# A transformer layer stack on one core: the products for the memory gates laid by token tiles on 32-column strips of the array, with the gates as a block diagonal

## The chip, the core and the metric

The kernel runs on one core of a Trainium2 chip. A core has five engines that work side by side, each on its own in-order queue of instructions: TensorE (PE in the profile; PEld are its weight loads), VectorE (DVE), ScalarE (ACT), GpSimd (POOL) and SyncE (SP), which here only issues DMAs. They share an on-chip memory of 128 partitions, and TensorE writes its products into a second memory, PSUM, from which the other engines read. The metric is the device time of one execution in microseconds; the median of three runs of the kernel before is 1268.3 us.

## The reference

x has 8 batches of 512 tokens with 256 features. Four blocks follow each other, each with a layernorm ahead of it and a residual sum behind it: attention with a memory term, a feed-forward block, a retention block, the feed-forward block again.

```python
x = x + attn_a(layernorm(x))
x = x + ffn(layernorm(x))
x = x + attn_b(layernorm(x))
x = x + ffn(layernorm(x))
```

The change is in the first block. Its attention has 16 heads of 16 features, keys and values from a latent of 64 features, rope on queries and keys, and a decay by distance inside the softmax. What matters here is the memory term:

```python
memory_k = mean(k, axis=2)                     # one key per head
memory_v = mean(v, axis=2)                     # one value per head
memory_scores = einsum('bhqd,bhkd->bhqk', q, memory_k)
out = out + 0.2 * sigmoid(memory_scores) * memory_v
... out @ Wo + bo
```

For each batch there are thus 16 gates per token (one per head), and 16 memory rows, one per head, which are multiplied by Wo once.

## The kernel before

The work of one batch is cut into the front (layernorm, latent, keys, queries, values, the memory), the attention itself, and the rest (Wo, feed-forward, retention, feed-forward). All arithmetic is in 32-bit floats; a matmul is two rows of the trace.

**The attention** runs in 256 score steps, 32 per batch: a step makes the scores of a query tile of 128 tokens for two heads (s, in score_item) and VectorE takes their row maxima (mr); twelve steps later (LAG) the transposed scores (t, in prob_item) are made, ScalarE takes the exponential into p, and VectorE or GpSimd multiplies p by the decay table dec_a (soft_item; one pair of instructions a step). The products with the values (pv, in pv_item) have 128 rows and 32 columns of the array each, four heads side by side. Two score banks of PSUM (ps_sc) serve s and t, three others (ps_m) all other products.

**The memory.** mean_k (L533) puts the mean key into kmean as 16 columns, one per head. gate (L540) multiplies kmean by the rotated queries: two products of 512 columns each, one for each half of the rope, into rows 0 to 15 of a bank, and takes a tanh into the gates (a sigmoid is half of 1 + tanh). mean_v (L443) scales vmask, which has a column per head and one column of ones, by the mean value into vmean; through_wo (L458) multiplies it by Wo into mem, whose row 16 carries all that doesn't depend on a token: the output bias, and half of the memory rows. In the gates, row 16 is a constant 1, loaded once from the rope table. In wo_unit (L733), the product of gates and mem is the third product of each token tile, after the two of the attention's output with Wo:

```python
for c in range(NC):
    mm(ps[:, e * D : (e + 1) * D], aT[b][:, c, cols], wo_sb[:, c, :], c == 0, False)
mm(ps[:, e * D : (e + 1) * D], gates[b % 2][:, cols], mem[b % 2], False, True)
```

It has 128 rows of the array, of which only 17 hold anything but zeros.

**The order.** Ahead of the loop, the setup is written out by hand (from L1026). From there a planner (plan, L1072) decides when each piece comes. Each piece is a Unit with the time that it is booked for on TensorE and on the engines behind it; gate is Unit(gate, 1720, (("ACT", 600),)). The planner walks through the score steps with a clock for each engine, chooses at each point a step, a pair of value products or a Unit, and sums up the gaps of TensorE. It does so for all combinations of six rules (L1393: among them how long the decay product waits for GpSimd rather than go to VectorE, and how many steps earlier a front begins), takes the cheapest, and only then emits instructions, all engines in program order. In the first 64 steps it fills a gap of TensorE of over 700 ns with matmuls on the identity (warm), whose result nobody reads:

```python
if t < 2 * PER and gap > 700 and banks[0] <= clock["PE"] and not any(spare[i] for i in ts):
    n = min(20, (gap - 300) // 109)
    ...
    if emit:
        warm(n)
```

So a Unit's cost can change the order of the whole kernel. The decay product is given to GpSimd or VectorE by the line `pooled[i] = on <= own + (lead if i < EARLY else bias)` (L1232), where lead and bias are two of the rules.

## Time and profile before

| | us |
|---|---|
| three runs | 1267.91, 1268.30, 1269.02 |
| the profiled execution, its own time | 1267.68 |
| its span in the trace | 1265.9 |
| ACT busy | 499.4 |
| DVE busy | 615.4 |
| POOL busy | 763.6 |
| warm (fill) matmuls, 152 rows, length of one row, median | 0.275 |
| ga: 32 rows (8 gates), start to end of one row, median | 0.592 |
| tanh of a gate on ScalarE, 16x512, median | 0.587 |
| wo from me and ga: 64 rows, one row, median | 0.379 |

A row of the trace that gives a matmul's length counts from its start to its end, and the next one begins before it has ended; what a matmul costs is read from start to start. The span is what the trace covers; the device time lies some 1.8 us above it. Busy times of engines overlap, so they don't sum to the span.

### The profile page before, as it was taken

The numbers are of one execution on the slowest core, as the hardware profiler recorded it, in microseconds if no ns is written. First come the engines' busy times: TensorE is split into PE (matmuls) and PEld (weight loads), VectorE is DVE, ScalarE is ACT, GpSimd is POOL, SyncE is SP. The second block draws the span as 40 slices with busy tenths as digits, with TensorE's granted clock in tenths as the row PEclk, the third lists the DMA queues.
The fourth block names the chain that finished last, engine by engine and source line by source line (L and its number), as shares of the span: only waits on it lengthen the run. The fifth ranks groups of instructions, "written<-read, shape, count | busy, mean of one in ns | idle before, by whom it ended". The sixth has DMA issues, their size and how long they took to land.

```text
span 1265.9 us, 15939 instructions
## 1 busy us (share of the span) xinstructions
PE 1225.4 (97%) x6168; PEld 628.8 (50%) x6168; DVE 615.4 (49%) x995; ACT 499.4 (39%) x746; POOL 763.6 (60%) x699
## 2 busy tenths in 40 slices
PE   7989999999998999999999999999999999999999
PEld 5423445344534344455443644535543554467777
DVE  4777854573544663345734365433634372232410
ACT  2245444444453434334335245343434334523131
POOL 4379965795766876676657576675656564731210
PEclk9999999999999999999999999999999999999999
DMA  5310010002100100010000200011000100000000
GB/s 136 117 39 23 23 38 6 14 7 56 29 14 5 49 23 18 18 48 23 1 14 5 66 22 14 1 31 41 4 5 14 31 5 5 26 1 1 1 5 30
DMA packets 32728, 31.94 MB, mean 25 GB/s; under 512 B 14065, under 2 KB 23538, under 8 KB 32372
## 3 DMA queue, kind: packets, MB, share of 16 engines
q1 hardware_dynamic: 31740, 30.13, 8.7%
q8 instruction: 49, 0.80, 0.3%
q10 hardware_dynamic: 912, 0.79, 0.2%
q14 instruction: 27, 0.22, 0.1%
HBM read 13.92 MB, written 4.43 MB: 14 GB/s over the span
## 4 chain that ended last, share of the span: by engine, by line
PE 88%; DVE 6%; POOL 2%; DMA 2%; ACT 1%; issue 1%; SPq 0%; ACTq 0%; DVEq 0%
PE hx L203 19%; PE s L203 18%; PE x L203 18%; PE pv L203 8%; PE wo L203 3%; PE bs L203 3%; PE bo L203 3%; DVE mr L69 3%; PE b L203 2%; PE bv L203 2%; PE q L203 2%; POOL p L69 2%; PE t L203 2%; PE warm L203 1%; PE lat L203 1%; PE ga L203 1%
## 5 line engine op out<-in xcount | busy, mean ns | idle before, releaser
L69 POOL TENSOR_TENSOR p<-p,dec_a 128x512 f32<-128x512 f32 x482 | 610.0, 1290 | 296.5 <-ACT p L69 290.1
L69 DVE TENSOR_REDUCE mr<-s 128x2 f32<-128x1024 f32 x256 | 312.7, 1223 | 314.0 <-PE t L203 291.6
L69 ACT ACTIVATE p<-t 128x1024 f32<-128x1024 f32 (+1 forms) x282 | 263.0, 944 | 366.0 <-PE t L203 356.3
L203 PE MATMUL s<-kT,qT 32*128 32x512 f32 x1024 | 289.3, 640 | 19.5 <-DVE mr L69 17.0
L203 PE MATMUL t<-qT,kT 32*128 32x512 f32 x1024 | 287.2, 641 | 0.5 <-ACT p L69 0.3
L203 PE MATMUL x<-w_sb,h_x 128*128 128x256 f32 x960 | 221.0, 384 | 0.0
L203 PEld LDWEIGHTS x<-w_sb,h_x 128*128 128x128 f32 x960 | 178.3, 190 | 59.4 <-issue 36.4
L203 PEld LDWEIGHTS s<-kT,qT 32*128 32x128 f32 x1024 | 78.0, 183 | 162.0 <-DVE mr L69 62.9
L203 PE MATMUL pv<-p,va 128*32 128x512 f32 x1024 | 132.8, 608 | 1.6 <-ACT num L69 0.7
L69 ACT ACTIVATE h_x<-hx,vec 128x512 f32<-128x512 f32 (+1 forms) x128 | 84.5, 660 | 109.2 <-PE hx L203 108.3
L203 PE MATMUL hx<-xT_f,w_sb 128*128 128x512 f32 (+1 forms) x288 | 122.1, 560 | 0.2 <-ACT xT_f L69 0.2
L203 PE MATMUL hx<-xT_g,w_sb 128*128 128x512 f32 (+1 forms) x288 | 122.0, 560 | 0.0
L69 DVE TENSOR_TENSOR x<-x,x 128x256 f32<-128x256 f32 x60 | 25.5, 425 | 153.2 <-PE x L203 145.7
L203 PEld LDWEIGHTS t<-qT,kT 32*128 32x128 f32 x1024 | 78.6, 183 | 14.2 <-ACT p L69 5.4
L203 PEld LDWEIGHTS hx<-xT_g,w_sb 128*128 128x128 f32 x288 | 51.2, 189 | 64.0 <-issue 60.1
L203 PEld LDWEIGHTS hx<-xT_f,w_sb 128*128 128x128 f32 x288 | 50.8, 189 | 64.3 <-issue 55.3
L203 PEld LDWEIGHTS pv<-p,va 128*32 128x32 f32 x1024 | 25.3, 109 | 77.1 <-issue 51.5
L69 POOL TENSOR_TENSOR x<-x,b 128x256 f32<-128x256 f32 x60 | 43.9, 754 | 14.7 <-DVE xn_g L69 11.6
L69 POOL TENSOR_TENSOR rc<-rc,rs 128x512 f32<-128x512 f32 x30 | 40.2, 1361 | 9.2 <-DVE rs L69 9.2
L69 DVE TENSOR_TENSOR p<-p,dec_a 128x512 f32<-128x512 f32 x30 | 35.7, 1227 | 18.1 <-ACT p L69 18.1
L69 POOL TENSOR_TENSOR rstd_g<-ve_g,half 128x2 f32<-128x2 f32 x16 | 11.3, 704 | 54.0 <-DVE ve_g L69 53.8
L69 ACT COPY num<-pv 128x512 f32<-128x512 f32 x32 | 18.7, 585 | 57.9 <-PE pv L203 53.4
(172 smaller groups left out, 1103.0 us busy)
## 6 DMA issues: line engine op xcount, KB each, us to landing
kT<-rc SPq DMA_DIRECT2D x64, 64.0 KB
qT<-rc SPq DMA_DIRECT2D x60, 64.0 KB
x<-in_x_dram SPq DMA_DIRECT2D x7, 512.0 KB
aT<-num SPq DMA_DIRECT2D x112, 32.0 KB
rec<-d_rec SPq DMA_DIRECT2D x14, 256.0 KB
out_dram<-x SPq DMA_DIRECT2D x28, 128.0 KB
w_sb<-in_w_dram SPq DMA_DIRECT2D x2, 1024.0 KB
x<-in_x_dram SPq DMA_DIRECT2D x2, 256.0 KB
```

The source lines that it names most:

```text
L69: ins = f(*a, **k)
L203: tc.keep_in_program_order(nc.tensor.matmul(o, lhsT=l, rhs=r, start=start, stop=stop))
```

## The change

The products for the gates are cut by token tiles. For each half of the rope and each of the four tiles of 128 tokens there is one product with kmean, which now has 32 columns, and the result of tile t goes to partitions 32t to 32t+31 of the bank, its columns to 0 to 127. The tanh is taken tile by tile into the gates so that tile t stands in rows 32t to 32t+31 and columns 128t to 128t+127: a block diagonal, zero elsewhere. The memory's rows stand in mem four times, at rows 32t, so that the product in wo_unit (unchanged) still finds its gates and rows. For this, vmask, vmean and bo_row repeat their content four times, and vmean's scaling covers 128 columns instead of 17. The row of ones comes from the tanh itself: a bias of 40 in row 16 of each strip (one_rows, made from a table that lies in memory) gives tanh(40) = 1; the two loads of the gates' row of ones go. bo_row is loaded into four rows. mem needs no zeros beforehand, since its addition now writes all 128 rows. pick, which is only used at the start, moves to a buffer of the p pool. The Unit of the gate is booked with 620 ns on TensorE and 900 on ScalarE.

```diff
-    bo_row = keep([32, D], "bo_row")
-    kmean = keep([P, 2, P], "kmean")
+    one_rows = keep([P, 4], "one_rows")
+    bo_row = keep([P, D], "bo_row")
+    kmean = keep([P, 2, 32], "kmean")
-    vmask = keep([P, NC, NH + 1], "vmask")
+    vmask = keep([P, NC, NT, 32], "vmask")
...
             gps.memset(gates[i], 0.0)
-            gps.memset(mem[i], 0.0)
...
         gps.tensor_scalar(hmask, hmask, 0.5 / T, None, ALU.mult)
+        for t in range(1, NT):
+            gps.tensor_copy(vmask[:, :, t, :NH], vmask[:, :, 0, :NH])
...
-        for i in range(2):
-            move(gates[i][NH : NH + 1, :], rope[HD : HD + 1, 0, :])
+        move(one_rows, blocks[:, P : P + 4])
...
-        move(bo_row[NH : NH + 1, :], rows[D : 2 * D].unsqueeze(0))
+        move(bo_row[NH:P:32, :], rows[D : 2 * D].partition_broadcast(NT))
...
-    pick = keep([P, 2, 32], "pick")
+    pick = at.tile([P, 2, 32], F32, tag="p", bufs=PB, name="pick")
...
-                gps.tensor_scalar(vmean[:, c, : NH + 1], vmask[:, c, :], m[:, c : c + 1], None, ALU.mult)
+                gps.tensor_scalar(vmean[:, c, :], vmask[:, c].rearrange("p t h -> p (t h)"), m[:, c : c + 1], None, ALU.mult)
...
-            dve.tensor_add(mem[b % 2][: NH + 1, :], ps[: NH + 1, :D], bo_row[: NH + 1, :])
+            dve.tensor_add(mem[b % 2], ps[:, :D], bo_row)
...
             for e in range(2):
-                mm(ps, kmean[:, e, :], rot[0, e], e == 0, e == 1)
-            act.activation(gates[b % 2][:NH, :], ps[:NH, :], AF.Tanh)
+                for t in range(NT):
+                    mm(
+                        ps[t * 32 : t * 32 + 32, :P], kmean[:, e, :], rot[0, e][:, t * P : (t + 1) * P],
+                        e == 0, e == 1,
+                    )
+            for t in range(NT):
+                own = slice(t * 32, t * 32 + 32)
+                act.activation(gates[b % 2][own, t * P : (t + 1) * P], ps[own, :P], AF.Tanh, bias=one_rows[own, 0:1])
...
-        ga = Unit(gate, 1720, (("ACT", 600),), after=[km, qt], needs=(("wo", b - 2),))
+        ga = Unit(gate, 620, (("ACT", 900),), after=[km, qt], needs=(("wo", b - 2),))
...
-    gps.tensor_copy(vmean[:, :, NH], bvc)
+    gps.tensor_scalar(one_rows, one_rows, 40.0, None, ALU.mult)
+    dve.reduce_sum(one_rows[:, 0:1], one_rows, axis=AX.X)
+    for t in range(NT):
+        gps.tensor_copy(vmean[:, :, t * 32 + NH], bvc)
```

More of the change, by code (lines that the diff above doesn't have):

```diff
@@ L167, in memory_buffers @@
         gps.memset(vmask, 0.0)
-        gps.memset(vmask[:, :, NH : NH + 1], 1.0)
+        gps.memset(vmask[:, :, :, NH : NH + 1], 1.0)
         gps.memset(kmean, 0.0)
@@ L174, in masks @@
             dve.reduce_sum(
-                vmask[:, c, c * HH : (c + 1) * HH], ident.rearrange("p (h d) -> p h d", d=HD), axis=AX.X
+                vmask[:, c, 0, c * HH : (c + 1) * HH], ident.rearrange("p (h d) -> p h d", d=HD), axis=AX.X
             )
         gps.tensor_scalar(hmask, hmask, 0.5 / T, None, ALU.mult)
+        for t in range(1, NT):
+            gps.tensor_copy(vmask[:, :, t, :NH], vmask[:, :, 0, :NH])
     late = {}
@@ L455, in bias_through_wo @@
                 mm(ps[:, :D], vmean[:, c, :], wo_sb[:, c, :], c == 0, c == NC - 1)
-            dve.tensor_add(bo_row[: NH + 1, :], ps[: NH + 1, :D], bo_row[: NH + 1, :])
+            dve.tensor_add(bo_row, ps[:, :D], bo_row)
         def through_wo():
```

## The prediction

> **What bounds the kernel now.** I read the page first: the engines' shares, then the chain of waits.

> ```profile
> PE 1225.4 (97%) x6168; PEld 628.8 (50%) x6168; DVE 615.4 (49%) x995; ACT 499.4 (39%) x746; POOL 763.6 (60%) x699
> ...
> PE 88%; DVE 6%; POOL 2%; DMA 2%; ACT 1%; issue 1%; SPq 0%; ACTq 0%; DVEq 0%
> ```

> TensorE is busy 97% of the span and owns 88% of the chain, so a microsecond taken off it should be a microsecond of the total. But the share is a mean over stages, so I cut the span at the score steps (one score tile each, 256 in all, read from the row maxima on VectorE): step 12 at 57 us, step 48 at 161, step 74 at 272, last step at 1087.

> ```profile
> 57.40:95.00 37.60, 31.18 (x162) 10.18 (x154) 28.38 (x31) 16.52 (x31) 28.89 (x26) 0.95 0.13 33
> 95.00:130.00 35.00, 32.52 (x193) 11.00 (x194) 27.93 (x35) 18.64 (x33) 31.89 (x28) 1.00 0.11 29
> 130.00:161.00 31.00, 30.18 (x183) 13.15 (x182) 24.19 (x28) 15.89 (x30) 27.84 (x22) 1.00 0.07 18
> 161.00:272.00 111.00, 108.33 (x573) 51.13 (x571) 62.59 (x107) 47.51 (x65) 76.36 (x69) 1.00 0.07 17
> 272.00:1134.00 862.00, 847.26 (x4250) 412.88 (x4249) 407.47 (x647) 356.26 (x492) 565.83 (x503) 1.00 0.08 21
> ```

> The columns are the stretch, its length, and busy time of PE, PEld, DVE, ACT and POOL. From 161 us on TensorE is idle 2%. In the three front rows it is idle 6.4 + 2.5 + 0.8 = 9.7 us of 103.6, and POOL (88.6) and DVE (80.5) are nearly as loaded: there the engines pace each other. The waits of TensorE name the maxima on VectorE first (17.0 us, 22 times, for the next score tile).

> **The gates' products.** The third view is the timeline of TensorE around one gate.

> ```profile
> 332.71 0.59 PE L203 MATMUL s<-kT,qT 32*128 32x512 f32 x2
> 332.72 0.59 PE L203 MATMUL t<-qT,kT 32*128 32x512 f32 x2
> 333.24 1.98 PE L203 MATMUL ga<-rc,kmean 128*128 128x512 f32 x4
> 335.16 1.92 PE L203 MATMUL pv<-p,va 128*32 128x512 f32 x16
> ```

> A gate holds the array 1.92 us (333.24 to 335.16): two products, two rows each. Eight cost 15.4 us. Afterwards a gate is 8 products of 128 columns, 16 rows, in the shape of pv (128 rows, 32 columns), where four lie side by side: 16 pv rows of 512 columns take 1.86 us, so four at once take 0.46. A quarter of the columns is 0.12, four rounds 0.46, and entering a new shape costs 0.2 (a lone pair hx of 4 rows takes 1.91 us, 8 rows in a row 3.63). That gives **0.65 us**. Ends: 0.43 (pure streaming), and 16 x 0.112 = 1.8 if the four tiles run one after the other. The floor on issue is the nearest row with such small tiles:

> ```profile
> 4.81 0.84 PE L203 MATMUL qk_bias<-vec,pick 128*32 128x1 f32 x32
> 5.58 0.38 PE L203 MATMUL warm<-ident 128*128 128x128 f32 x1
> ```

> 32 rows in 0.77 us are 24 ns each, 16 make 0.39, less than the streaming. [...] The row is for the same tile shape, so I take 24 ns. Saving: 1.92 - 0.65 = **1.27 us a gate**. Gate 0 counts: the maximum after it waits 2.19 us for its score tile where its neighbours wait 0.47. Gate 1 (near 101 us) lies in a stretch that I find paced by VectorE below, so I count seven: **-8.9 us**.

> **The order around them.** The gate's cost enters the planner (1720 to 620), and the built order shows that it now chooses other rules. TensorE's work is the same but for two counts: fill matmuls on the identity go from 76 to 125, and changes of array shape from 609 to 618. The last batch's work from its first wo on comes in the same order, so the last 131 us should not change. Of the decay products (p times dec_a, two for each step) 60 instead of 30 are on VectorE; of those of the first 36 steps, 20 steps' instead of 7.

> Fills. Before, 14 stand after score step 46 and 3 after 61. After: 15, 4, 14, 9, 13, 7, 4, after steps 24, 45, 46, 49, 50, 52, 61. What one costs is in this timeline:

> ```profile
> 152.75 3.29 PE L203 MATMUL warm<-ident 128*128 128x128 f32 x28
> ...
> 153.39 1.21 DVE L69 TENSOR_REDUCE mr<-s 128x2 f32<-128x1024 f32 x1
> ...
> 155.97 0.19 PEld L203 LDWEIGHTS s<-kT,qT 32*128 32x128 f32 x2
> ```

> 28 rows are 14 matmuls, 0.224 us each, where the planner books 109 ns. The maximum that frees the score bank ends at 154.60; the scores start at 155.97, behind the fill: 1.37 of its 3.13 us is loss. 49 more fills are 11.0 us of TensorE, of which 45% (4.9) delays by that measure, and the rest stands for idle time, which is loss too where the old order had work there.

> Decay products. The tile view has one, and the timeline how two engines meet:

> ```profile
> L69 DVE TENSOR_TENSOR p<-p,dec_a x30: 677/1196/1765, 65.7 to 1111.1; 128x512 f32<-128x512 f32 x30
> ```

> ```profile
> 81.65 3.42 DVE L69 TENSOR_TENSOR p<-p,dec_a 128x512 f32<-128x512 f32 x2
> 82.80 3.40 POOL L69 TENSOR_TENSOR p<-p,dec_a 128x512 f32<-128x512 f32 x2
> ```

> Beside a busy POOL a pair takes VectorE up to 3.4 us and stretches POOL's own pair from 2.5 to 3.4; the shortest is 0.68 each. In steps 12 to 47 the order puts 40 of them on VectorE instead of 14. With POOL lighter by 13 pairs (32 us of 88.6) I take 0.97 each, between the floor and the median: 26 x 0.97 = 25 us more, VectorE 80.5 to about 106, in a stretch of 103.6. It is in-order and cannot be busy all the time: a step whose decay product stays on POOL costs 2.33 at least (maximum 1.16, then 1.17 for the next scores to be made), one with both on VectorE 1.16 + 1.94. Steps 12 to 35: 15 x 3.1 + 9 x 2.33 + about 8 of rope and layernorm = 75.5, against some 72 now; the last third is near its old length plus the fills. With in-order waits: **+7.5 us** (ends: 0 with the floor, +14 with the median). The 19 fills there lie inside it. Steps 48 to 74 are TensorE's: 30 fills are 6.7 us, less idle that they replace (2.7 us in that row): **+5** (2.5 to 6.7).

> **The small edits.** Nine shape changes more, 0.2 each by the hx rows: +1.8. The tanh goes from one of 0.59 to four: the nearest row, neg from PSUM, 16x128, is 0.27, so 1.1, +0.5 each on ACT, 39% busy, and it holds a bank of PSUM as long; the wo that reads it comes a batch later: 0, or 0.5 a gate without that cover. The vmean products grow from 17 to 128 columns, 0.35 to about 0.45 (one blocked beside VectorE took 1.2), hidden except before me: +0.1. Setup: two memsets of me less (0.31 each); one_rows' small DMA takes the place of two rows of the gates on SP's queue ahead of bvc; POOL waits 6.8 us for bvc anyway, then makes four copies of 0.19 instead of one ahead of kmean, which gate 0 needs 17 us later. VectorE's sum of one_rows waits there too, with only the first maximum (33.6) behind it: 0, at worst 0.5. The pick tile takes a decay buffer that nothing wants until later: 0. The additions onto me and bo_row keep 256 columns: 0.41 as now.

> **Sum.** -8.9 + 7.5 + 5 + 1.8 = +5.4. The profiled execution took 1267.7 (span 1265.9), 0.6 under the median of 1268.3. So **1273 us**, slower by 0.4%. For 272 to 1134 I assume the same 15 us of idle time in another order, +-4.

> **The rivals.** *The cover holds* (faster): VectorE's products run near 0.68 as POOL is free, the front keeps its length, the fills stand where TensorE would wait anyhow (+2.5). Then (gate 1 saves too) -10.2 + 2.5 + 1.8 = -5.9: 1262 us. For it: the front rows leave VectorE 23 us idle. Against: 0.68 is the minimum of 30, and TensorE is 91% busy there. The switch is at about 0.75 us a product. *VectorE paces the front* at today's median 1.2 and every fill is loss: -8.9 + 14 + 6.7 + 1.8 = +13.6: 1281 us. For it: 82.80 shows that both engines suffer. *The tiles do not lie side by side*: a gate stays near 1.9 and the rest remains, +14.3: 1282 us; pv's rows speak against it.

> **How the numbers follow.** Main case 0.48 (1268 to 1278 by itself), cover holds 0.31, VectorE paces 0.15, tiles serial 0.06. 0.2% (2.5 us) is about what a measurement tells from no change. Of the main case, 0.36 is slower beyond it, 0.10 within, 0.02 faster; of the faster rival 0.26 faster, 0.05 within; the other two are slower. Together: faster 0.28, within 0.15, slower 0.57. The range cuts both tails: 1258 to 1284.

> **What would show it.** [...] Front: step 48 comes later than 161 us, near 167, VectorE over 90% busy from 57 us, its p rows between 0.9 and 1.1. Fills: behind each the score tile starts the moment the fill ends, with the maximum done before. Step 74 near 281. After it, each gate gains 1.27. I am wrong if step 48 is on time or early, or if the middle's idle time moves by over 5 us.

## The result, and the profile after

The changed kernel takes 1277.57 us (median of four runs, 1275.26 to 1278.34); the kernel before took 1268.11 beside it. The ratio is 1.0078 [1.0066, 1.0091]: slower by 9.5 us, where 5.4 were forecast. The profiled execution took 1278.34 us, its span is 1276.5.

From the page of the changed kernel, the engines' shares and the chain of waits:

```profile
PE 1235.2 (97%) x6362; PEld 640.8 (50%) x6362; DVE 638.2 (50%) x1029; ACT 502.3 (39%) x765; POOL 731.6 (57%) x674
...
PE 87%; DVE 7%; POOL 2%; ACT 1%; issue 1%; DMA 1%; SPq 0%; DVEq 0%; ACTq 0%; POOLq 0%
```

TensorE is as dominant as before, and busy 9.8 us longer. That is not its work: the eight gates take 10.7 us less than before (0.58 us for 1.92), and 49 fills more, at 0.224 us, take 11.0 us. Cut at the same score steps (12, 24, 36, 48, 74, then the rest but for the tail; columns as before, and the number behind POOL's count is the granted clock of TensorE):

```profile
54.40:102.90 48.50, 41.36 (x199) 13.72 (x191) 35.45 (x43) 18.35 (x35) 22.14 (x19) 0.82 0.10 26
102.90:136.20 33.30, 29.78 (x187) 11.24 (x187) 30.67 (x44) 14.83 (x26) 16.98 (x14) 0.96 0.05 14
136.20:172.80 36.60, 34.56 (x203) 14.52 (x200) 28.75 (x36) 16.45 (x32) 18.74 (x14) 0.89 0.06 16
172.80:287.00 114.20, 112.87 (x637) 57.37 (x636) 57.56 (x103) 47.94 (x68) 72.87 (x68) 1.00 0.06 17
287.00:1145.00 858.00, 842.08 (x4311) 412.00 (x4311) 420.68 (x659) 359.03 (x503) 568.25 (x503) 1.00 0.08 21
```

Steps 12 to 48 take 118.5 us instead of 103.4. VectorE, which was to pace them, is busy 94.9 of them: 80%, not over 90. What had not been in the sum stands in the clock column: 0.82, 0.96 and 0.89 where the kernel before had 0.98 over the stretch. From step 48 on the clock is full.

How far each step lies behind the kernel before, by the start of its row maximum in the two profiled executions, and how the difference grew, against the forecast's terms:

| step | before, us | after, us | difference | grown by | forecast |
|---|---|---|---|---|---|
| 0 | 33.6 | 31.7 | -1.9 | -1.9 | 0 |
| 12 | 57.4 | 54.4 | -3.0 | -1.1 | -1.3 (gate 0) |
| 48 | 160.8 | 172.8 | +12.1 | **+15.1** | +7.5 |
| 74 | 271.4 | 287.0 | +15.6 | +3.5 | +3.7 (fills 5, gate 2) |
| 255 | 1087.3 | 1098.1 | +10.8 | -4.8 | -4.6 (five gates, shape changes) |
| end of span | 1265.9 | 1276.5 | +10.6 | -0.2 | 0 |

The first line is no effect of the change: in the eleven later kernels that have the changed setup, step 0 comes between 32.8 and 34.9. One term is off, by a factor of two; that the -4.6 came out is partly luck, as order_alone will show.

Inside it, TensorE's timeline of the changed kernel (start, length, what, and in brackets the idle time before it and who ended that):

```profile
85.13 5.75 PE L205 MATMUL q<-xT_a,wq_sb 128*128 128x512 f32 x8
...
131.26 0.62 PE L205 MATMUL t<-qT,kT 32*128 32x512 f32 x2
134.66 1.22 PE L205 MATMUL s<-kT,qT 32*128 32x512 f32 x2 [2.78 <-DVE mr L69]
...
137.72 1.94 PE L205 MATMUL pv<-p,va 128*32 128x512 f32 x8
```

and VectorE's at the same place:

```profile
129.43 1.16 DVE L69 TENSOR_REDUCE mr<-s 128x2 f32<-128x1024 f32 x1
130.50 2.96 DVE L69 TENSOR_TENSOR p<-p,dec_a 128x512 f32<-128x512 f32 x2
133.39 1.21 DVE L69 TENSOR_REDUCE mr<-s 128x2 f32<-128x1024 f32 x1
```

A decay pair of 2.96 us stands between two maxima, the scores wait 2.78 us for the second, and then the rows on TensorE take longer: a score pair 1.22 instead of 0.70, eight pv rows 1.94 instead of 1.06, eight rows of q 5.75 at 85 us instead of 3.70. From start to start, whole-array rows of 512 columns take 0.85 us there and 0.43 elsewhere in this trace. That is a half clock, 0.50 in the view below (the q rows ran at it for most of their time). There are four such episodes in steps 12 to 48, 27.3 us in all, where the kernel before has one, of 3.41 us at 76.33. In the view of stretches, the four and then the 3.41 us ahead of the third:

```profile
58.57:68.81 10.24, 9.69 (x32) 2.65 (x28) 7.37 (x10) 2.28 (x4) 4.15 (x5) 0.50 0.00 0
82.46:89.29 6.83, 6.83 (x13) 2.35 (x8) 5.54 (x7) 3.50 (x8) 3.25 (x4) 0.50 0.30 78
133.66:140.49 6.83, 5.83 (x24) 1.96 (x28) 6.51 (x7) 1.59 (x3) 4.82 (x4) 0.50 0.02 8
154.14:157.55 3.41, 3.41 (x20) 0.72 (x16) 2.40 (x3) 1.08 (x2) 0.28 (x1) 0.50 0.00 0
130.25:133.66 3.41, 1.24 (x8) 0.41 (x8) 3.41 (x4) 1.09 (x2) 3.41 (x3) 1.00 0.22 65
```

So the clock did not wait here for the end of the pause: it fell at 133.66, 1.0 us before the scores started, when TensorE had been busy for 1.24 of the last 3.41 us.

### The profile page after: what moved, and what is told of

Its sections match the earlier page's. It is cut to its first block, busy times and chain, and to the rows that moved or that the text cites. A ratio compares the mean times of both kernels' runs of the same rounds, so it can differ in the third digit from the quotient of the medians.

```text
span 1276.5 us, 16335 instructions
## 1 busy us (share of the span) xinstructions
PE 1235.2 (97%) x6362; PEld 640.8 (50%) x6362; DVE 638.2 (50%) x1029; ACT 502.3 (39%) x765; POOL 731.6 (57%) x674
## 4 chain that ended last, share of the span: by engine, by line
PE 87%; DVE 7%; POOL 2%; ACT 1%; issue 1%; DMA 1%; SPq 0%; DVEq 0%; ACTq 0%; POOLq 0%
PE s L205 19%; PE x L205 18%; PE hx L205 18%; PE pv L205 9%; DVE mr L69 3%; PE bs L205 3%; PE wo L205 3%; PE bo L205 3%; PE b L205 2%; PE warm L205 2%; PE bv L205 2%; PE q L205 2%; PE t L205 2%; DVE p L69 1%; PE lat L205 1%
## 5 line engine op out<-in xcount | busy, mean ns | idle before, releaser
L69 POOL TENSOR_TENSOR p<-p,dec_a 128x512 f32<-128x512 f32 x452 | 572.5, 1289 | 320.7 <-ACT p L69 317.7
L69 DVE TENSOR_REDUCE mr<-s 128x2 f32<-128x1024 f32 x256 | 312.9, 1223 | 306.2 <-PE t L205 291.2
L69 ACT ACTIVATE p<-t 128x1024 f32<-128x1024 f32 (+1 forms) x283 | 263.2, 941 | 389.4 <-PE t L205 387.4
L205 PE MATMUL s<-kT,qT 32*128 32x512 f32 x1024 | 292.3, 647 | 17.2 <-DVE mr L69 17.0
L205 PE MATMUL t<-qT,kT 32*128 32x512 f32 x1024 | 293.9, 650 | 2.0 <-DVE bo_row L69 1.5
L69 ACT ACTIVATE h_x<-hx,vec 128x512 f32<-128x512 f32 (+1 forms) x128 | 84.5, 660 | 109.9 <-PE hx L205 109.9
L69 DVE TENSOR_TENSOR x<-x,x 128x256 f32<-128x256 f32 x60 | 25.5, 425 | 145.0 <-PE x L205 133.8
L69 DVE TENSOR_TENSOR p<-p,dec_a 128x512 f32<-128x512 f32 x60 | 54.8, 951 | 21.1 <-ACT p L69 21.1
L69 POOL TENSOR_TENSOR x<-x,b 128x256 f32<-128x256 f32 x60 | 44.2, 760 | 17.8 <-DVE xn_g L69 9.4
L69 POOL TENSOR_TENSOR rstd_g<-ve_g,half 128x2 f32<-128x2 f32 x16 | 11.3, 704 | 62.8 <-DVE ve_g L69 62.5
L69 POOL TENSOR_TENSOR rc<-rc,rs 128x512 f32<-128x512 f32 x30 | 39.7, 1344 | 6.4 <-DVE rs L69 6.4
L205 PEld LDWEIGHTS warm<-ident 128*128 128x128 f32 x250 | 32.3, 206 | 12.9 <-issue 9.9
```

Source lines behind the costliest of these rows:

```text
L69: ins = f(*a, **k)
L205: tc.keep_in_program_order(nc.tensor.matmul(o, lhsT=l, rhs=r, start=start, stop=stop))
```

## The experiments

A hypothesis came first out of the traces: **the clock theory.** Shorter work and longer waits on TensorE let its clock fall to half, and that is what the forecast lacks. Its rivals: the order alone does it (VectorE's decay products, as forecast), or the longer fills do.

A note on all times below. The runs of one kernel spread over several microseconds, along a line with the mean granted clock of the run: fitted within the kernels, 0.87 us for 0.001 of clock. An episode of 3.41 us at half clock is 0.0013 of the mean clock, 1.2 us on this line. So beside a median I give the mean moved along that line to a clock of 0.995, about that of the kernel before (0.9946, 1268.35 us, so 1268.0). That is my calculation, not a measurement: gates_alone has 1270.53 at 0.987, and 0.87 x 8 less is 1263.6. The changed kernel has 1277.2 at 0.9902, so **1273.1**: at equal clock it is 5.1 us slower, and the clock makes the other 3.8.

**The gates without their new order.** The unit keeps its old booking, so the planner chooses the order of before.

```diff
-        ga = Unit(gate, 620, (("ACT", 900),), after=[km, qt], needs=(("wo", b - 2),))
+        ga = Unit(gate, 1720, (("ACT", 600),), after=[km, qt], needs=(("wo", b - 2),))
```

> All edits of the change but the planner is booked the old 1720/600 for a gate, so the order is the old one with only the gates' products exchanged. If the loss is the new order's (both the clock theory and the fill theory), this is faster than before: 8 gates x (1.92 - 0.58) = 10.7 us off on TensorE, 1268 to about 1258 (1256 to 1261), step 48 at about 157 us, granted clock 0.99 as before. If the gates' own edits cost (four tanh, wider vmean, a block diagonal), it is no faster than 1268.

Measured: 1270.28, ratio 1.0018 [1.0005, 1.0031]. Eight gates, each 1.34 us shorter, in an unchanged order, gain nothing. The timeline of TensorE shows where one went:

```profile
465.36 0.64 PE L205 MATMUL ga<-rc,kmean 128*32 128x128 f32 x16
465.93 0.60 PE L205 MATMUL mv<-lsum,wv_sb 64*128 64x1 f32 x4
466.46 1.98 PE L205 MATMUL hx<-xT_g,w_sb 128*128 128x512 f32 x4
472.15 0.95 PE L205 MATMUL s<-kT,qT 32*128 32x512 f32 x2 [3.71 <-ACT p L69]
...
474.73 3.78 PE L205 MATMUL hx<-xT_g,w_sb 128*128 128x512 f32 x4
```

The same gate in the kernel before, on TensorE:

```profile
462.72 1.98 PE L203 MATMUL ga<-rc,kmean 128*128 128x512 f32 x4
...
469.57 1.13 PE L203 MATMUL s<-kT,qT 32*128 32x512 f32 x4 [2.41 <-ACT p L69]
...
471.20 1.98 PE L203 MATMUL hx<-xT_g,w_sb 128*128 128x512 f32 x4
```

The scores come 6.85 us after the gate's start before, and 6.79 with the short gate. The wait has swallowed the saving (2.41 to 3.71), and the longer wait is followed by hx rows of double length. What the scores really wait for is in the kernel before, on ScalarE and on VectorE:

```profile
467.52 1.09 ACT L69 ACTIVATE xn_f<-x,nm_f,rstd_f 128x256 f32<-128x256 f32 x2 [7.38 <-DVE nm_f L69]
468.51 1.00 ACT L69 ACTIVATE p<-t 128x1024 f32<-128x1024 f32 x1
```

```profile
461.76 0.69 DVE L69 TENSOR_TENSOR x<-wo,x 128x512 f32<-128x512 f32 x1 [1.96 <-PE wo L203]
466.25 0.75 DVE L69 BATCH_NORM_STATS2 st_a<-x 128x6 f32<-128x256 f32 x2 [3.79 <-DMA x<-in_x_dram]
...
467.33 0.15 DVE L69 SCALAR_TENSOR_TENSOR nm_f<-mv_f,rstd_f 128x2 f32<-128x2 f32 x1
```

Read from the end: the scores need a bank that the exponential p frees; p is behind xn_f on ScalarE; xn_f needs nm_f; nm_f is behind the statistics st_a on VectorE; and these wait 3.79 us for the load of another batch's x, which starts when the residual sum at 461.76 has freed its buffer. This gate stood in the shadow of a transfer (the other seven were not followed back like this). In the changed kernel VectorE waits for a load of x once ahead of st_a, for 0.7 us.

**The order without the gates.** The kernel before, with the new booking.

```diff
-        ga = Unit(gate, 1720, (("ACT", 600),), after=[km, qt], needs=(("wo", b - 2),))
+        ga = Unit(gate, 620, (("ACT", 900),), after=[km, qt], needs=(("wo", b - 2),))
```

> The old gates with the new booking 620/900: the changed kernel's order with the old products. If the order alone loses, about 1277.6 + 10.7 = 1288 (1284 to 1290; less if the gates in the front hide), with the same half-clock episodes before step 48 (mean clock near 0.88 there). If the loss came with the gates, about 1268.

Measured: 1284.46, ratio 1.0129 [1.0114, 1.0144]; step 48 lies 11.4 us behind, step 74 16.3, and 20.5 us of steps 12 to 48 have the half clock already with the old gates. The order costs 16 us and the gates take back 7 of them, of the 10.7 that they save on TensorE. The loss comes from two numbers in a planner's table.

This run also takes the -4.6 of the forecast apart. From step 74 to 255, at full clock in both, the old gates in the new order gain 1.5 us on the kernel before (16.3 to 14.8 behind), and the short gates another 3.3 (15.6 to 10.8 is 4.8 in all). The forecast had 6.35 for these five gates and lost 1.8 of it to shape changes. Both terms were off, and the errors cancelled.

**The planner's second choice.** Booked sums of the two best orders differ by 0.2 us in 1265; the second gives GpSimd up to 3 us of patience for an early decay product (lead 3000 instead of 0).

```diff
-    plan(*min(rules, key=cost.get), emit=True)
+    plan(90000, 0, 0, 1, 3000, 3000, emit=True)
```

> The changed kernel with the planner's rule fixed to its second choice, which differs from the first in one rule: lead 3000 instead of 0, so that early decay products wait for GpSimd. 28 decay products on VectorE instead of 60, 95 fills instead of 125. Clock theory: with VectorE free the maxima come in time, TensorE doesn't fall to half clock in steps 12 to 48, step 48 near 160 instead of 173, in all about 1263 to 1268. Fill theory: 30 fills less x 0.224 x 0.45 = 3 us: 1274. Theory that GpSimd paces: no gain, 1277.

Measured: 1271.97, ratio 1.0023 [1.0000, 1.0045]; at equal clock 1267.8. Step 44 is on time (+1.1), so an order with the early products on GpSimd does not lose the front; then 20 fills in one place and 12 products of wo moved forward put step 48 at +13.5, of which 8.1 are given back by step 255.

**Shorter fills.** In the changed kernel, 109/224 of each stretch of fills that the planner puts in; those of the setup and of the first steps stay.

```diff
-                    warm(n)
+                    warm(max(1, n * 109 // 224))
```

> The changed kernel's order with each fill cut to n x 109/224 matmuls, so that it lasts as long as the planner books: 125 becomes 87. Fill theory: 38 x 0.224 = 8.5 us less of TensorE, and all of it is won back where it held up the scores, so up to -8 us and at least -4: 1270 to 1274, with the gain after step 24 and after step 48. Clock theory: the gain is smaller than that in steps 12 to 48, as TensorE waits more and its clock may fall more often; by it alone 1275 to 1278.

Measured: 1274.71, ratio 1.0048 [1.0032, 1.0065]: 2.9 us less than the changed kernel. A fill does cost 0.22 us, and part of it is on the path, in the changed kernel's timeline:

```profile
183.88 0.64 PE L205 MATMUL ga<-rc,kmean 128*32 128x128 f32 x16
184.46 0.60 PE L205 MATMUL mv<-lsum,wv_sb 64*128 64x1 f32 x4
184.99 2.27 PE L205 MATMUL warm<-ident 128*128 128x128 f32 x18
187.19 0.70 PE L205 MATMUL s<-kT,qT 32*128 32x512 f32 x2
```

Nine fills (18 rows) take 2.20 us, booked 0.98, and the scores start as they end. The first two lines are also the gate itself: 0.58 us from its start to the next.

**Is it the clock?** Four kernels. Three keep the order of before and vary what the gate leaves TensorE to do: six whole-array products on the identity behind it, its own products three times over, or identity products only in the grown waits. The fourth puts identity products into the four waits of the changed kernel's front.

```diff
@@ gates_filled, in gate(), ahead of the tanh
+            for j in range(6):
+                mm(ps[:, P + j % 3 * P : 2 * P + j % 3 * P], ident, ident)
@@ gates_thrice, in gate()
-            for e in range(2):
+            for e in (0, 1) * 3:
@@ gates_waits, before or after the products of a step behind gates 2, 3 and 4
+                for j in range(waits["n"]):
+                    mm(waits["ps"][:, P + j % 3 * P : 2 * P + j % 3 * P], ident, ident)
@@ front_filled, in step()
+    FRONT = {19: 7, 36: 9, 42: 6}
...
+                if t in FRONT:
+                    warm(FRONT[t])
...
+                    if t == 13 and k == 2:
+                        warm(5)
```

> The gates' new products in the order of before, and six products of the identity with itself (128x128, 0.22 us each by the fills' rows) behind each gate's sixteen rows, in columns of its bank that nothing reads: TensorE is as long at a gate as before (0.58 + 1.34 = 1.92 us), and works on the whole array in it. Clock theory (the shorter gate costs time because the wait behind it grows and TensorE's clock falls to half after it): the wait behind the gate near 465 goes from 3.7 back to about 2.4 us, the mean clock from about 0.986 back to 0.995, the time to 1266 to 1268. Rival, another of the change's parts costs it (four tanh rows in place of one, the wider sums and rows): the clock may come back, the time stays at 1270 or rises to 1272.

> The gates' new products in the order of before, run three times over in each gate (the result is the same): 48 rows on 32 columns each, 3 x 0.58 = 1.74 us, so that the wait behind a gate is nearly what it was before, but the gate stays work on 32 columns at a time. If the clock falls because the waits grew, the mean clock comes back to about 0.995 and the time to 1267 to 1268.5. If it falls because the products on 32 columns count for less with the clock's control than whole-array ones, the clock stays near 0.986 and the time at 1270 or above.

> The gates' new products in the order of before, and products of the identity only in the waits that grew: nine (2.0 us) in the wait of 2.95 us near 340, nine in that of 3.71 near 470, five (1.1 us) in that of 1.7 us near 174. They add 5.2 us of TensorE's work where it stood idle. Clock theory: the episodes of half clock near 174, 342 and 472 go (that near 600 is left), mean clock 0.993 or more, time 1264 to 1267, so below before. Waits alone, without the clock: the work fits in the waits, time unchanged at 1270. Work on the path: 1272 to 1275.

> The changed kernel, and products of the identity in the four waits that precede half clock in its front: five (1.1 us) within step 13, seven before step 19, nine before step 36, six before step 42; 27 in all, 6 us of TensorE's work more. Clock theory: the clock of steps 12 to 48 rises from 0.88 to 0.95 or more, step 48 comes 6 to 10 us earlier (from +12 to between +2 and +6 against before), and the time falls from 1277.6 to 1268 to 1272. VectorE theory (the 40 decay products it does there pace the stretch, whatever the clock): step 48 stays at +12 or goes to +15, time 1277 to 1280.

And later, a fourth length of the gate, two halves of 256 tokens instead of four tiles of 128:

```diff
-                for t in range(NT):
+                for t in range(2):
                     mm(
-                        ps[t * 32 : t * 32 + 32, :P], kmean[:, e, :], rot[0, e][:, t * P : (t + 1) * P],
+                        ps[t * 32 : t * 32 + 32, : 2 * P], kmean[:, e, :], rot[0, e][:, 2 * t * P : 2 * (t + 1) * P],
```

> The gates in the order of before, in two halves of 256 tokens on 32 columns each in place of four tiles of 128: eight rows of 256 columns, two side by side, an estimated 4 x 0.28 = 1.1 us (0.58 with four, 1.92 in before), and two tanh rows of 32x256, an estimated 2 x 0.43 = 0.87 us of ScalarE (1.44 with four, 0.59 in before). If ScalarE's longer tanh is what eats the saving behind the gates, this keeps more of it than four tiles did: 1266 to 1268. If the shorter TensorE work and the clock are what costs, it lies between before and four tiles: 1268.5 to 1270, at a mean clock between 0.987 and 0.995.

All kernels of this table have the order of before; the gate's length is from start to start, fills included:

| kernel | gate, us | median, us | ratio to before | mean clock | mean us moved to clock 0.995 |
|---|---|---|---|---|---|
| before | 1.92 | 1267.5 to 1268.9 | | 0.9946 | 1268.0 |
| gates_filled | 2.1 | 1269.39 | 1.0018 [1.0005, 1.0030] | 0.9937 | 1268.9 |
| gates_thrice | 1.33 to 1.45 | 1270.96 | 1.0020 [1.0011, 1.0030] | 0.9904 | 1266.2 |
| gates_waits | 0.46 to 0.57 | 1271.18 | 1.0021 [1.0010, 1.0032] | 0.9900 | 1266.2 |
| gates_halves | 0.88 to 0.99 | 1271.15 | 1.0020 [1.0011, 1.0030] | 0.9874 | 1264.5 |
| gates_alone | 0.46 to 0.57 | 1270.28 | 1.0018 [1.0005, 1.0031] | 0.9870 | 1263.6 |

Without the two with added identity products the order is plain: the shorter the gate, the less time at equal clock, and the lower the clock. The two cancel, and all times are alike within a microsecond or two. Three gates' surroundings in gates_alone, and then in gates_filled, in the view of stretches, with the clock third from the end:

```profile
330.00:350.00 20.00, 16.69 (x114) 7.85 (x113) 16.57 (x35) 11.25 (x19) 16.67 (x18) 0.91 0.11 28
460.00:480.00 20.00, 16.29 (x81) 7.12 (x84) 10.07 (x28) 9.43 (x17) 14.28 (x17) 0.83 0.08 27
580.00:610.00 30.00, 29.39 (x151) 14.31 (x149) 16.91 (x32) 13.85 (x23) 19.83 (x20) 0.89 0.09 23
```

```profile
330.00:350.00 20.00, 17.72 (x128) 8.98 (x127) 15.95 (x35) 11.70 (x20) 16.71 (x18) 1.00 0.12 28
460.00:480.00 20.00, 17.62 (x99) 9.25 (x98) 10.26 (x27) 9.44 (x17) 13.44 (x16) 0.91 0.10 27
580.00:610.00 30.00, 28.68 (x176) 15.83 (x175) 19.00 (x36) 15.23 (x25) 21.18 (x21) 1.00 0.09 23
```

Work that nobody reads brings the clock back here (0.91 to 1.00, 0.83 to 0.91, 0.89 to 1.00), as the clock theory said. That gates_filled took 1269.39 and not 1266 to 1268 is not settled: with the six products its gate is 0.19 us longer than before's, 1.5 us over eight, near the 1.9 by which it lies above the kernel before; the four tanh rows are another suspect. The halves were to tell whether ScalarE's tanh, 1.44 us with four tiles, eats the saving: they shorten it and gain nothing, so there is no sign of it. gates_waits failed in one place through its own making. At the wait near 470 its nine products came to stand behind the gate's tanh, as the timeline of its TensorE shows:

```profile
469.85 4.21 PE L205 MATMUL ga<-ident 128*128 128x128 f32 x18 [5.16 <-ACT ga L69]
473.99 1.22 PE L205 MATMUL s<-kT,qT 32*128 32x512 f32 x2
```

They waited 5.16 us and then ran at half clock ahead of the scores, 4.2 us on the path (18 such rows took 2.27 at 184.99 in the changed kernel). That decides nothing between the theories. Near 340, where they ran in the wait, the clock is 1.00 (0.91 in gates_alone).

front_filled took 1278.04, ratio 1.0086 [1.0058, 1.0115], no better than the changed kernel. Its stretches:

```profile
57.00:100.00 43.00, 37.44 (x208) 15.11 (x206) 31.86 (x39) 17.36 (x34) 19.78 (x18) 0.92 0.09 23
100.00:130.00 30.00, 29.23 (x187) 11.70 (x188) 27.07 (x42) 14.76 (x26) 11.93 (x11) 1.00 0.07 15
130.00:173.00 43.00, 39.76 (x255) 17.56 (x257) 37.81 (x43) 18.65 (x35) 25.75 (x22) 1.00 0.07 20
```

Most of the clock is back (one episode of 6.83 us is left), and from step 0 to 48 it takes 136.6 us, where the changed kernel took 141.1 and the one before 127.2. So of the 13.9 us lost there, some 4.5 went with the clock, net of what the 27 products cost, and **9.4 stay at nearly full clock**. That is one execution of each, and this one has the highest clock of its four (0.997; two had 0.991 and 0.992 and took 1283.1 and 1280.5). The clock theory is a third of the loss in the front, and its time of 1268 to 1272 is missed.

Why so little comes back, a sum of TensorE's time in steps 12 to 48 of the three traces shows. The products are the same there but for the gate's and the fills. "Lost to half clock" is half of the busy time in the episodes, and a fill is put at 0.224 us; both are my estimates.

| steps 12 to 48, us | before | after | front_filled |
|---|---|---|---|
| length | 103.4 | 118.5 | 113.9 |
| TensorE idle | 9.7 | 12.7 | 9.6 |
| fills | 3.1 | 7.4 | 13.4 |
| lost to half clock | 1.7 | 12.9 | 3.3 |
| the rest | 88.8 | 85.5 | 87.6 |

By this the half clock takes 11.2 us more of TensorE's time than before, of the 15.1 by which the stretch grew. In front_filled 9.6 of it are gone, yet the stretch is only 4.6 shorter: idle time and fills have grown by 2.9 and the rest by 2.1. So a part of the rows at half clock had run in time in which TensorE would else have waited. What is left of the loss, 10.5 us, is nearly all idle time and fills (23.0 where the kernel before has 12.8).

**Is the rest VectorE's load?** The changed kernel's order, with 19 early decay pairs moved to GpSimd; and the same with shorter fills, this time with every fill of the kernel cut.

```diff
                 prob_at[i] = clock["POOL" if pooled[i] else "DVE"] = on if pooled[i] else own
+                if emit and i < 36:
+                    pooled[i] = on <= own + 3000
@@ early_pooled_short_fills, in addition, in warm()
-        for j in range(n):
+        for j in range(max(1, n * 109 // 224)):
```

> The changed kernel in its own order on TensorE, ScalarE and SyncE; alone the engine of the early decay products is chosen again: a product of the steps up to 47 goes to GpSimd where the planner's clocks put it at most 3 us later there, which moves 19 pairs from VectorE to GpSimd. VectorE theory (those pairs delay the row maxima and so the steps, 9 us of the 14 that steps 0 to 48 lose at full clock): step 48 comes 8 to 12 us earlier than in the changed kernel (from +12 to between 0 and +4 against before), with fewer waits of TensorE for a maximum and so less half clock, time 1266 to 1271. Rival, the order on TensorE itself, or the clock, loses it: step 48 stays at +9 to +13, time 1275 to 1279.

> Both repairs at once: the early decay products on GpSimd as in the run beside it, and each stretch of fills at 109/224 of its length. If the two losses are separate and add, the time is the one beside it less 3 us (what shorter fills gave alone): 1263 to 1268, at or below the kernel before. If shorter fills only bring back waits and half clock, it equals the one beside it or is above it.

Measured: 1283.74, ratio 1.0116 [1.0087, 1.0146], step 48 at +14.2; and 1291.16, ratio 1.0173 [1.0147, 1.0198]. Both miss on the far side. In the first, VectorE is lighter by 21 us in steps 12 to 48 (74.1 busy), GpSimd heavier by 43 (100.5 against 57.9), and the wait has only moved. VectorE's timeline, then one line of GpSimd's and one of TensorE's:

```profile
59.12 2.15 DVE L69 TENSOR_SCALAR xn_a<-x,mv_a,rstd_a 128x256 f32<-128x256 f32 x2
61.18 1.21 DVE L69 TENSOR_REDUCE mr<-s 128x2 f32<-128x1024 f32 x1
62.32 2.71 DVE L69 TENSOR_SCALAR xn_a<-x,mv_a,rstd_a 128x256 f32<-128x256 f32 x2
```

```profile
57.35 7.53 POOL L69 TENSOR_TENSOR p<-p,dec_a 128x512 f32<-128x512 f32 x6
65.15 2.07 PE L205 MATMUL t<-qT,kT 32*128 32x512 f32 x2 [4.09 <-DVE mv_a L69]
```

Beside six decay rows in a row on GpSimd, a pair of layernorm rows takes 2.15 and 2.71 us on VectorE, and TensorE waits 4.09 us for what is behind it. So taking products off VectorE does not help by itself: this order is worse with another assignment, and lead_3000, built for GpSimd from the start, is on time at step 44. Which waits of the order make up the 9.4 us stays open; the fills ahead of step 48 (92 instead of 73, 4.3 us) are in it.

The second shows something else, and says nothing on the sum of the two repairs, since short_fills had left the fills of the first steps alone. Here they fall from two to one behind each of these steps. This is the stretch of steps 0 to 12, first with two (early_pooled), then with one, and TensorE's timeline with one:

```profile
34.00:57.00 23.00, 23.00 (x129) 11.18 (x128) 17.04 (x23) 5.20 (x18) 3.58 (x5) 1.00 0.51 173
34.00:57.00 23.00, 23.00 (x55) 8.40 (x54) 10.89 (x9) 2.67 (x12) 2.81 (x3) 0.52 0.50 174
```

```profile
38.73 2.08 PE L205 MATMUL s<-kT,qT 32*128 32x512 f32 x4
40.73 0.80 PE L205 MATMUL warm<-ident 128*128 128x128 f32 x2
41.46 2.08 PE L205 MATMUL s<-kT,qT 32*128 32x512 f32 x4
```

TensorE is busy for 23.00 of 23.00 us in both, and with one fill the clock is 0.52 all the same. It had fallen at 35.14, behind a wait of 2.84 us for a DMA; over the next 43 us, from 57 to 100, it is 0.78 (0.88 in early_pooled).

**A version with all of it.** The second order, and the planner told that a fill takes 224 ns.

```diff
-                n = min(20, (gap - 300) // 109)
+                n = min(20, int(gap - 300) // 224)
...
-                banks.append(clock["PE"] + n * 109)
+                banks.append(clock["PE"] + n * 224)
...
-    plan(*min(rules, key=cost.get), emit=True)
+    plan(90000, 0, 0, 1, 3000, 3000, emit=True)
```

> The changed kernel with the planner's second choice of order (lead 3000, which puts nearly all early decay products on GpSimd; alone it gave 1272.0) and each stretch of fills booked, and so counted out, at the 224 ns that a fill takes in place of 109: 19 fewer fills (10 of them before step 48), 4.3 us less of TensorE's time. If the fills' overshoot is on the path: 1268 to 1270, which is the kernel before within what can be measured. If the granted clock falls for want of them, or the steps only wait for longer: 1271 to 1274.

Measured: 1268.54, ratio 0.9998 [0.9985, 1.0012]: within the expected 1268 to 1270, and no different from the kernel before. Its mean clock is 0.9917; moved to 0.995 its mean would be 1265.1. No version here beats the kernel before by a margin that can be measured.

## Why the prediction was right, and where it was not

The direction, the outline of the mechanism (a cheaper gate changes the order, and the order costs more than the gates give) and the range held. By its steps:

- **The gate: right, its worth not.** 0.58 us against 0.65 forecast (1.92 before). In gates_thrice 48 rows take 1.33 us, 28 ns each, near the 24 of the row that was chosen. But a gate was to gain its full 1.27 us after step 74, and it gains about half: 3.3 us for five in the new order, 4.4 for eight at equal clock in the old one (gates_alone).
- **The front, +7.5: the term that was mis-sized.** It measured +15.1, and not in the way that was forecast. The step had VectorE pace the stretch: 26 decay products more at 0.97 us, 25 us, busy over 90%. They took 0.87 each, VectorE's load grew by 14.4 us, and it was busy 80%. TensorE's idle time and fills grew by 7.3 us, about the size put down, but the sum had no term for TensorE's clock, at half of which 25.8 us of its work ran (3.4 before). Some 4.5 us come back with the clock (front_filled). The rest, 9 to 10, is above 7.5 but within the ends that were given (0 to 14). That the decay products on VectorE are its cause is not shown: taking them away in the same order made it worse.
- **Fills behind step 48, +5: right.** Steps 48 to 74 grew by 3.5 with gate 2's 1.3 gained inside, and by 4.9 with the old gates (order_alone). The price of 0.22 us a fill holds, as does the sign that scores start when a fill ends.
- **Shape changes, +1.8: not seen.** In the new order with the old gates the long stretch is 1.5 us shorter than before (order_alone). With the gates' 3.3 that gives the 4.8 against 4.6 forecast, by luck.
- **Idle time and the tail: right.** In the long stretch TensorE is idle 15.9 us (14.7 before), within the 4 that were allowed; the last part changed by 0.2.
- **The small edits: no loss found in the changed kernel.** The four tanh rows are 0.36 each, 1.44 in all against 1.1 forecast. vmean's scaling is 0.61 instead of 0.36, forecast 0.45.
- **The rivals.** The cover did not hold (step 48 late). "VectorE paces the front" came near in size (14 there) but not in mechanism. The tiles do lie side by side: 16 rows in 0.58 us are 36 ns each, where a fill's row of as many columns takes 112.

The front was 7.6 us worse than forecast and the total only 4: step 0 came 1.9 us early in the profiled execution, and the medians lie 9.5 us apart where the two profiled executions lie 10.7. Neither is an effect that the forecast had.

## What to carry to other kernels

A saving on the busiest engine is worth what the next wait leaves of it: read which instruction ends that wait, and follow it back over the queues until you find what it really depends on, here often a transfer or a layernorm on another engine. Where a planner decides the order, a changed cost is a changed kernel: build the new order with the old instruction, and the old order with the new one, and price them apart. Put the granted clock beside every stretch before you price rows in it: at half clock four hx rows took 3.78 us here instead of 1.98, and filler work gave back some 4.5 us net in the front of front_filled, while shorter fills saved 2.9 (short_fills).

## What the runs showed of the hardware

What lies ahead of a change is an estimate of mine, a sum over each such window of these two traces (364 in each, from 10 to 1255 us): of each matmul row its length at full clock (0.43 us for 512 columns, less in proportion) times the share that its shape in the trace (`32*128`, `128*32`) has of the largest one there, `128*128`, divided by 3.41 us. The windows ahead of the 8 falls have 0.02 to 0.35, and of the 706 windows at full clock that are followed by another, one has 0.35 and the rest 0.38 or more. The 4 windows at half clock that are followed by another have 0.16 to 0.29, and the 8 ahead of a return 0.44 to 0.51. At half clock the busy share does not separate them: in two of the 4 TensorE was busy all the time. The score products with one fill behind each group give 0.24 at half clock (four score rows and two of a fill in 2.73 us, from 38.73 in early_pooled_short_fills); with two, at full clock, they give 0.51 (31 to 45 us in the changed kernel).

The mean clocks of the gates' versions go the same way. By this sum a gate counts 1.71 us in the kernel before and in gates_filled, 1.28 in gates_thrice, and 0.43 both in two halves and in four tiles, whatever its length; the mean clocks are 0.9946 and 0.9937, 0.9904, 0.9874 and 0.9870. The sum was fitted to traces, and no run was built to test it: that the clock goes by it is not shown.

**VectorE and GpSimd took longer beside each other.** A layernorm pair takes 0.73 us on VectorE near 455 us in the kernel before, while GpSimd does nothing for most of it, and 2.15 to 2.71 beside GpSimd's decay products in early_pooled:

```profile
455.68 0.73 DVE L69 TENSOR_SCALAR xn_g<-x,mv_g,rstd_g 128x256 f32<-128x256 f32 x2
```

GpSimd's own decay product takes 1.26 us with no decay product on VectorE beside it (126.89 in the changed kernel), and 1.46 each in the four (5.83 us from 129.99) that meet VectorE's pair of 2.96 us.
